# Two rows of attention factors: from TensorE transposes to small transfers through DRAM

## The chip, the cores and the metric

The kernel runs on one core of a Trainium2 chip. The metric is the device time of one execution in microseconds (us); less is better. Before the change it is 2583.25 us, the median of 3 runs from 2581.5 to 2585.15. The profiled execution has a span of 2584.1 us.

A core has five engines with a queue each: TensorE (PE: matmuls and transposes, into PSUM), VectorE (DVE), ScalarE (ACT), GpSimd (POOL) and SyncE (SP, which here only issues transfers). An engine runs its queue in order, and an instruction at its head that waits for a semaphore holds up all behind it. Transfers run on 16 DMA engines.

## What is computed

The input x is 32 graphs of 512 nodes with 256 features, in fp32, with one adjacency matrix for all. Per graph two layers follow each other, both added to x:

```
# layer 1, on layernorm(x):
out = relu(x @ mlp1_w + mlp1_b);  residual = out
out = elu(gat(relu(out), None, W_fc, a_fc)) + residual
out = relu(out @ mlp2_w + mlp2_b);  residual = out
out = relu(elu(gat(relu(out), adj, W_hand, a_hand)) + residual)
# where
def gat(inp, adj, W, a):
    h = inp @ W
    f1 = h @ a[:F, 0];  f2 = h @ a[F:, 0]
    e = leaky_relu(f1[:, :, None] + f2[:, None, :], 0.2)
    if adj is not None: e = where(adj > 0, e, -9e15)
    return elu(einsum('bij,bjf->bif', softmax(e, axis=2), h))
# layer 2, on layernorm(x): per head, softmax weights of 64 slices, sums of the
# nodes by them, attention among the 64 slice tokens, and back to the nodes
```

What matters here are f1 and f2, one number for each node. Matmuls leave them as a column: node on the partition, four tiles of 128 nodes. The matrix e needs one of the two as a column, and the other as a row of 512 that is the same on all 128 partitions. Getting from the column to that row is what the change is about.

## The kernel before, in words

The kernel handles the 32 graphs one after the other. A graph b passes through `front` (line 650), `middle` (757) and `back` (850), whose parts have names: load, norm1, mlp1, h, factors, p, pv, o1 (front); mlp2, h2, e, p2, pv2 (middle); norm2, w, sums, s1T, tokens, att, vo, gg, out (back). Parts of up to four graphs run at the same time, each in another stage.

The order of the queues is not the order of the program text. A `Recorder` takes every instruction down with a cost, and `order` plans them: each part has a due time in `TURNS`, and the instruction that can start and is due first goes next. `HEAD` and `TAIL` shift the due times of the first and last three graphs. `ISSUE`, `BEGIN`, `LAND`, `BEHIND` and `SWITCH` are what the plan takes for transfers and for changes of the matmul's shape. The resulting order is fixed; `emit` (line 281) issues it, so the profile gives line 283 for all, and one has to go by the tiles' names.

For graphs other than the first and last (`EDGES`), most transposes of big tiles don't go through TensorE. `flip` has VectorE transpose blocks of 32 × 32 into a stage, and `gather` (line 392) writes the stage to DRAM in four transfers and reads it back in one, all from SyncE's queue. In the first and last graph TensorE transposes them.

**factors** (line 682) and **p**: h comes with the columns f1 and f2. VectorE takes the maximum of f2 per partition (fm), TensorE transposes it, VectorE takes the maximum of that, f2m, over all nodes. Then sc = f1 + f2m (a column of 4 tiles), and TensorE spreads it: each of the four columns, repeated 128 times along the free axis, is transposed with the identity, which gives a row of 128 that is the same on all partitions. The row, in PSUM, is clamped twice, by VectorE and by ScalarE, into acb [128, 2, 512], and one exponential is taken of both halves. The column f1 in h is then overwritten by ones, so that the product pv gives the softmax's denominator as well. p builds pT, four tiles, with ScalarE multiplying and VectorE taking a maximum.

**pv**: TensorE multiplies pT with h. ELU follows, then `flip` and `gather` into o1T (o1), to which o0T is added, and mlp2 reads it.

**h2** (line 769): the second attention's h, with f1 and f2 in columns 256 and 257. TensorE spreads the four columns of f2 by transposes into PSUM as f2b. **e**: VectorE adds f2b, the column f1 and the mask, and goes on to leaky relu, the maximum and (ScalarE) the exponential; e is flipped and gathered into p2T (p2), and pv2 multiplies it with h2.

PSUM has five banks for matmuls (`mm`) and three for transposes (`tr`).

Of the kernel before, what the change touches and what calls it, by code (L numbers as in the profile page):

```python
# [7 lines left out]
F32 = mybir.dt.float32  # L8
I32 = mybir.dt.int32
AF = mybir.ActivationFunctionType  # L10
OP = mybir.AluOpType
# [2 lines left out]
ENGINES = ("tensor", "vector", "scalar", "gpsimd", "sync")  # L14

TURNS = {
    "load": -742.6, "norm1": -217.3, "mlp1": 743.3, "h": 847.3, "factors": 855.6, "p": 866.5,
    "pv": 872.7, "o1": 889.6, "mlp2": 900.8, "h2": 927.5, "e": 936.4, "p2": 556.1, "pv2": 977,
    "norm2": 1016, "w": 1035.7, "sums": 1041, "s1T": 1049, "tokens": 1120.9, "att": 78.2,
    "vo": 523.7, "gg": 243.7, "out": 1133,  # L20
}
PERIOD, SPARE = 91.72, 0.01

HEAD = (
    (243, -394, 14, 0, 2, 2, 38, -6, -57, -26, -306, -182, 126, -448, -107, 24, -145, -19, 984,
     -3, -394, 7),
    (-86, 191, -245, 43, 3, -49, 0, 187, -87, -24, 282, -45, 0, -140, -297, 924, -29, 7, 0, 21,
     -410, -757),
    (0, -12, 458, 33, 0, 23, -538, 0, -933, -32, 0, 724, -118, -26, -35, 487, -576, -1224, 125,
     0, -2, -1),  # L30
)
TAIL = (
    (9, -189, 0, 1, 0, 710, -45, -103, -26, -185, -41, 0, 510, -99, 6, 0, -90, 581, 0, 15, 209,
     0),
    (108, -81, 0, 1, -49, 31, -115, 202, -383, 0, 0, 6, 17, -64, 590, 1127, 26, -44, -68, 9,
     -11, 325),
    (207, 9, 610, 12, -3, 56, 140, -80, -21, 0, -139, -238, 66, 676, 2, -3, -3, 134, 14, 0, 68,
     -217),
)


# [4 lines left out]
P = 128  # L46
# [4 lines left out]
class Recorder:  # L51
# [2 lines left out]

    SIGNAL = 0.06
    DRAIN = 0.17
    ISSUE, BEGIN, LAND, BEHIND = 0.45, 1.2, 0.9, 2.7
    SWITCH = 0.14
    KEPT = 1
    AHEAD = 3  # L60

# [65 lines left out]
    def _cost(self, op, out, ins):  # L127


        def words(ap):  # L130
            return ap.size() // ap.ap[0][1]

        n = words(out)
        if op.method == "dma_start":
            side = next(ap for ap in (out, *ins) if ap.space != bass.MemoryType.DRAM)
            op.moving = out.size() * 4 / (215e3 if side.ap[0][1] <= P // 4 else 320e3)
            return self.ISSUE, 0.0
        if op.engine == "tensor":
            one = max(n / 1200 + 0.002, 0.109)
            if op.mode == (P, P // 2):  # L140
                one = max(n / 2400, 0.038)
            elif op.mode == (P // 2, P // 2):
                one = max(n / 4800, 0.022)
            return (one if op.method == "transpose" else 2 * one), self.DRAIN
        if op.engine == "scalar":
            pointers = sum(isinstance(op.kwargs.get(k), bass.AP) for k in ("bias", "scale"))
            return 0.06 + n / 1200 + 0.09 * pointers + 0.19 * ("accum_out" in op.kwargs), 0.12
        if op.engine == "vector":
            n = max([n] + [words(x) for x in ins])
            single = op.method in ("tensor_copy", "tensor_scalar")  # L150
            fast = single and all(x.space != bass.MemoryType.PSUM for x in ins)
            pointers = sum(words(x) == 1 for x in ins) if n > 1 else 0
            return 0.07 + n / (1920 if fast else 960) + 0.065 * pointers, 0.1
        if n < 16:
            return (0.1 if op.method == "memset" else 0.3 if op.method == "tensor_scalar" else 1.1), 0.1
        return 0.2 + n / (480 if op.method == "tensor_tensor" else 960), 0.1

    def _schedule(self, ops, key, spare):
# [35 lines left out]
        while len(done) < len(ops):  # L194
# [21 lines left out]
            if op.engine == "tensor" and op.mode != mode:  # L216
                t, mode = t + self.SWITCH, op.mode
            op.start, op.end = t, t + op.cost + op.lag
# [101 lines left out]
def adj_ffn_kernel(  # L320
# [26 lines left out]
    B, N, D = x.shape  # L347
    HID = mlp1_w.shape[1]
    HH = HID // 2
    NT = N // P  # L350
# [9 lines left out]
    nc = Recorder(tc.nc)  # L360
# [3 lines left out]
    dram = ctx.enter_context(tc.tile_pool(name="dram", bufs=1, space=bass.MemoryType.DRAM))  # L364

    def ts(i, n=P):
        return slice(i * n, (i + 1) * n)

    def new(name, shape, bufs=1, tag=None, dtype=F32):
        return sbuf.tile(list(shape), dtype, name=name, tag=tag or name, bufs=bufs)  # L370

    def mm_tile(shape):
        return psum.tile(shape, F32, tag="mm", name="mm", bufs=5)

    def tr_tile(shape):
        return psum.tile(shape, F32, tag="tr", name="tr", bufs=3)
# [4 lines left out]
    EDGES = (0, B - 1)  # L381
# [6 lines left out]
    def by_dma(what, b):  # L388

        return what in FLIPPED and b not in EDGES  # L390

    def gather(what, stage, dst):

        blocks, width = stage.shape[1:]
        scr = dram.tile([blocks, Q, P // Q, width], F32, name="scr", tag=f"scr_{what}", bufs=2)
        for a in range(P // Q):
            nc.sync.dma_start(
                scr[:, :, a, :].rearrange("c r j -> r c j"), stage[ts(a, Q), :, :]  # L400
            )
        nc.sync.dma_start(
            dst, scr.rearrange("(k c) r a j -> (c r) k (a j)", c=P // Q)
        )

    def swapped(cols):

        return cols.rearrange("p (t a i) -> p a t i", t=NT, i=Q)
# [7 lines left out]
    def small(name, shape):  # L416
        return new(name, shape, bufs=3)
# [8 lines left out]
    def load_x(b):  # L426
# [11 lines left out]
    ident = new("ident", [P, P])  # L438
    nc.gpsimd.memset(ident, 0.0)
    nc.gpsimd.affine_select(  # L440
        out=ident, in_=ident, compare_op=OP.not_equal, fill=1.0, base=0,
# [122 lines left out]
    for k in range(KD):  # L564
        pt = tr_tile([P, INNER])
# [33 lines left out]
    for p in range(NP):  # L599
        pv = mm_tile([P, D])  # L600
# [20 lines left out]
    def transpose_features(what, b, src, dst, swap):  # L621

        if by_dma(what, b):
            stage = new(what + "_stage", [P, D // Q, P], tag="stage4")
            for t in range(NT):
                flip(src[:, t, :D], stage[:, :, ts(t, Q)])
            gather(what, stage, dst)
            return
        for k in range(KD):
            pt = tr_tile([P, N])  # L630
            for t in range(NT):
                nc.tensor.transpose(pt[:, ts(t)], src[:, t, ts(k)], ident)
            if swap:
                nc.scalar.copy(dst[:, k, :].rearrange("p (a t i) -> p a t i", t=NT, i=Q), swapped(pt))
            else:
                nc.scalar.copy(dst[:, k, :], pt)
# [13 lines left out]
    def front(b):  # L650
# [21 lines left out]
        h = new("h", [P, NT, 2, HH + 1])  # L672
        for t in range(NT):
            for s in range(2):
# [4 lines left out]
                    )  # L679
                nc.scalar.copy(h[:, t, s, :], pm)  # L680
        f1, f2 = h[:, :, 0, HH], h[:, :, 1, HH]
        nc.step = "factors"

        fm = small("fm", [P, 1])
# [3 lines left out]
        f2m = small("f2m", [P, 1])  # L688
# [2 lines left out]


        beta = 1.0 - ALPHA
        sc = small("sc", [P, NT])
        nc.vector.tensor_scalar(sc, f1, f2m, None, op0=OP.add)
        ex = small("ex", [P, 2, NT])
        nc.vector.tensor_scalar(ex[:, 0], f2, f2m, None, op0=OP.subtract)
        nc.vector.tensor_scalar(ex[:, 1], f2, f2m, ALPHA, op0=OP.subtract, op1=OP.mult)
        nc.scalar.activation(ex, ex, AF.Exp)

        nc.vector.memset(f1, 1.0)

        pt = tr_tile([P, N])
        for i in range(NT):
            nc.tensor.transpose(pt[:, ts(i)], sc[:, i : i + 1].to_broadcast([P, P]), ident)
        acb = new("acb", [P, 2, N])
        nc.vector.tensor_scalar(acb[:, 0, :], pt, -beta, 0.0, op0=OP.mult, op1=OP.max)
        nc.scalar.activation(acb[:, 1, :], pt, AF.Relu, scale=beta)
        nc.scalar.activation(acb, acb, AF.Exp, scale=-1.0)

        nc.step = "p"
# [1 line left out]
        for j in range(NT):  # L713
# [5 lines left out]
                op0=OP.mult, op1=OP.max,  # L719
# [6 lines left out]
        for i in range(NT):  # L726
# [14 lines left out]
            pt = tr_tile([P, KH, P])  # L741
# [8 lines left out]
        if by_dma("u", b):  # L750
            gather("u", stage, o1T)
            for m in range(KH):
                o1 = o1T[:, m, :].rearrange("p (t a i) -> p t a i", t=NT, i=Q)
                nc.vector.tensor_tensor(o1, o1, swapped(o0T[:, m, :]), op=OP.add)
        return o1T

    def middle(b, o1T):
# [12 lines left out]
        h = new("h2", [P, NT, D + 2], tag="h" if b == B - 1 else None)  # L770
        for t in range(NT):
# [3 lines left out]
                    pm, o2T[:, k, ts(t)], wh[:, k, :], start=(k == 0), stop=(k == KD - 1)  # L775
                )
            nc.scalar.copy(h[:, t, :], pm)
        f2b = tr_tile([P, N])
        for j in range(NT):
            nc.tensor.transpose(f2b[:, ts(j)], h[:, j, D + 1 : D + 2].to_broadcast([P, P]), ident)  # L780
        if not by_dma("e", b):
            pt, f2b = f2b, new("f2b", [P, N], tag="acb")
            nc.scalar.copy(f2b, pt)
        nc.step = "e"
        pT = new("p2T", [P, NT, N], tag="pT" if b == B - 1 else None)
# [3 lines left out]
        for i in range(NT):  # L789
            e = new("e", [P, N], bufs=2)  # L790
# [11 lines left out]
            pt = tr_tile([P, NT, P])  # L802
# [7 lines left out]
        if by_dma("e", b):  # L810
            gather("e", stage, pT)
# [15 lines left out]
        for i2 in range(NT // 2):  # L827
            parts = []
            for s in range(2):
                i = 2 * i2 + s  # L830
# [218 lines left out]
    for b in range(B):  # L1049
        nc.age = b  # L1050
        back(b, middle(b, front(b)))
# [57 lines left out]
```

## Time and profile before

| | before |
|---|---|
| time, median of 3 | 2583.25 us |
| span of the profiled execution | 2584.1 us |
| TensorE busy | 2543.5 us (98%) |
| VectorE busy | 1992.3 us (77%) |
| ScalarE busy | 1075.3 us (42%) |
| GpSimd busy | 90.5 us (4%) |
| DMA moved | 375.9 MB, 145 GB/s on the mean |
| transposes of sc (f1; two more a graph by this name are the attention's) | 192 records, 43.9 us |
| transposes of h (f2) | 128 records, 24.2 us |
| clamp of acb by VectorE, from PSUM | 32 records, 692 ns each |
| clamp of acb by ScalarE, from PSUM | 32 records, 598 ns each |

How to read it: a matmul in fp32 shows as two records on TensorE, a transpose as one. Matmuls are pipelined, so the records overlap, and the busy time is the time in which one at least is in flight; what one costs the queue is the distance from its start to the next start. In the lists of groups and timelines, `out<-in` are the tiles' names without numbers: `tr<-ident,sc` is the transpose of sc by the identity. Waits are given as who waited, for whom, us in total, times, and the longest. In the list of transfers stand the issuing queue, how many, the size of one and the median us from the issue's start to the landing.

### The profile page before, as it was taken

The page shows a single profiled execution, that of the slowest core. Times are in us where ns is not written, and L with a number is a line of the kernel's source. Part 1 is how long each engine was busy: PE and PEld are TensorE (multiplying, and loading weights), DVE is VectorE, ACT ScalarE, POOL GpSimd, SP SyncE. Part 2 cuts the span into 40 slices and gives each one's busy share as a digit, 9 for nine tenths or more (in the row PEclk, how much of TensorE's full clock was granted, in tenths as well). Part 3 has the DMA queues.
Part 4 walks back from the last instruction along what each step waited for, and adds up shares of the span by engine and source line. Part 5 has one row for each costly group of instructions (what it writes and reads, how often), then busy time and mean ns, then how long its engine had stood idle before and what let it go on. Part 6 is the DMA issues. An engine that isn't in the chain of part 4 may idle for free.

```text
span 2584.1 us, 35267 instructions
## 1 busy us (share of the span) xinstructions
PE 2543.5 (98%) x12437; PEld 1863.3 (72%) x12437; DVE 1992.3 (77%) x4968; ACT 1075.3 (42%) x2009; POOL 90.5 (4%) x167
## 2 busy tenths in 40 slices
PE   7999999999999999999999999999999999999998
PEld 5777767776677777777776777767777677777776
DVE  6577777877778777788777788777887778877786
ACT  3443444433444334444334443344443344433442
POOL 0000000000000000000000000000000000000000
PEclk9999999999999999999999999999999999999999
DMA  5135455554455554555544555545545455554342
GB/s 177 53 87 153 114 156 171 155 163 128 136 176 162 157 149 124 168 172 150 162 133 138 175 161 158 147 122 171 164 148 160 124 155 171 155 165 137 114 123 82
DMA packets 465318, 375.90 MB, mean 145 GB/s; under 512 B 86004, under 2 KB 382068, under 8 KB 465142
## 3 DMA queue, kind: packets, MB, share of 16 engines
q1 hardware_dynamic: 463558, 372.59, 48.6%
q8 instruction: 99, 1.62, 0.3%
q10 hardware_dynamic: 1584, 1.05, 0.1%
q14 instruction: 77, 0.63, 0.1%
HBM read 198.45 MB, written 175.11 MB: 145 GB/s over the span
## 4 chain that ended last, share of the span: by engine, by line
PE 84%; DVE 7%; DMA 6%; ACT 1%; SPq 1%; issue 1%; POOL 0%; DVEq 0%; ACTq 0%
PE mm L283 81%; PE tr L283 3%; DMA o1T<-scr 2%; DMA scr<-u_stage 2%; SPq L283 1%; DVE s L283 1%; DVE s_stage L283 1%; DVE acb L283 1%; ACT acb L283 1%; DVE pT L283 1%; DVE u L283 1%; DMA w_raw<-scr 1%; DVE w L283 0%; DVE u_stage L283 0%; DMA p2T<-scr 0%
## 5 line engine op out<-in xcount | busy, mean ns | idle before, releaser
L283 PE MATMUL mm<-wfc,o0T 128*128 128x257 f32 x2048 | 509.8, 382 | 0.0
L283 PEld LDWEIGHTS mm<-wfc,o0T 128*128 128x128 f32 x2048 | 375.5, 189 | 141.7 <-issue 102.3
L283 PE MATMUL mm<-h,pT 128*128 128x257 f32 (+1 forms) x2048 | 462.1, 382 | 8.2 <-DVE pT L283 4.7
L283 PEld LDWEIGHTS mm<-h,pT 128*128 128x128 f32 x2048 | 383.2, 189 | 80.8 <-DVE pT L283 24.3
L283 ACT COPY h<-mm 128x257 f32<-128x257 f32 (+1 forms) x384 | 143.6, 374 | 375.9 <-PE mm L283 373.7
L283 PE MATMUL mm<-weff,xn2T 128*128 128x512 f32 x512 | 248.7, 592 | 0.6 <-ACT xn2T L283 0.6
L283 PE MATMUL mm<-xn,w 128*128 128x256 f32 x1024 | 247.5, 380 | 0.9 <-DVE ln_mv L283 0.8
L283 PE MATMUL mm<-xnT,w 128*128 128x512 f32 x512 | 239.1, 600 | 1.0 <-ACT m L283 0.6
L283 PE MATMUL mm<-o1T,w 128*128 128x512 f32 x512 | 227.6, 596 | 12.0 <-DVE o1T L283 10.5
L283 PE MATMUL mm<-h,p2T 128*128 128x257 f32 x1024 | 236.7, 380 | 1.1 <-DMA p2T<-scr 1.1
L283 PE MATMUL mm<-gg,wT 128*128 128x256 f32 x1024 | 237.5, 380 | 0.1
L283 PEld LDWEIGHTS mm<-gg,wT 128*128 128x128 f32 x1024 | 191.3, 190 | 40.3 <-issue 14.3
L283 PEld LDWEIGHTS mm<-h,p2T 128*128 128x128 f32 x1024 | 193.8, 190 | 30.8 <-DVE ln_mv L283 1.0
L283 PEld LDWEIGHTS mm<-xn,w 128*128 128x128 f32 x1024 | 185.1, 190 | 33.0 <-issue 3.9
L283 PEld LDWEIGHTS mm<-o1T,w 128*128 128x128 f32 x512 | 94.8, 190 | 128.2 <-issue 101.0
L283 ACT ACTIVATE u<-mm,rd 128x256 f32<-128x256 f32 x192 | 90.2, 470 | 217.9 <-DVE u_stage L283 85.9
L283 DVE STREAM_TRANSPOSE o_stage<-o2T 128x512 f32<-128x512 f32 x64 | 45.1, 708 | 160.3 <-ACT o2T L283 160.3
L283 DVE SCALAR_TENSOR_TENSOR e<-tr,h,mbias 128x512 f32<-128x512 f32 x120 | 86.6, 742 | 106.4 <-PE tr L283 106.3
L283 ACT ACTIVATE w<-w 128x512 f32<-128x512 f32 x128 | 80.7, 630 | 199.2 <-DVE w L283 199.2
L283 PEld LDWEIGHTS mm<-xnT,w 128*128 128x128 f32 x512 | 93.2, 191 | 83.4 <-issue 77.0
L283 ACT ACTIVATE m<-m 128x512 f32<-128x512 f32 x192 | 120.0, 625 | 66.9 <-DVE m L283 66.7
L283 DVE SCALAR_TENSOR_TENSOR u<-m,u 128x512 f32<-128x512 f32 x192 | 130.9, 682 | 18.8 <-ACT m L283 15.9
(140 smaller groups left out, 3466.0 us busy)
## 6 DMA issues: line engine op xcount, KB each, us to landing
scr<-xn_stage SPq DMA_DIRECT2D x240, 128.0 KB, 2.4
scr<-u_stage SPq DMA_DIRECT2D x120, 256.0 KB, 4.8
o1T<-scr SPq DMA_DIRECT2D x30, 1024.0 KB, 5.9
scr<-e_stage SPq DMA_DIRECT2D x120, 256.0 KB, 4.5
p2T<-scr SPq DMA_DIRECT2D x30, 1024.0 KB, 5.7
scr<-w_stage SPq DMA_DIRECT2D x120, 256.0 KB, 5.6
w_raw<-scr SPq DMA_DIRECT2D x30, 1024.0 KB, 5.6
x<-in_x_dram SPq DMA_DIRECT2D x32, 512.0 KB, 6.1
```

Of the source, the lines that this page charges most:

```text
L283: getattr(getattr(self.nc, op.engine), op.method)(*op.args, **op.kwargs)
```

## The change

The row f1b is no longer made by TensorE from sc, and f2b no longer by TensorE from h2, in the 30 graphs that are not first or last. A new helper, `spread`, issues two transfers from ScalarE's queue: the column of 512 words goes to a line in DRAM, and the line is read back by all 128 partitions at once. The second waits for the first to land. f1b is spread as soon as h is there, without f2m. f2m is added when VectorE clamps: one op on f1b makes −0.8 (f1 + f2m), and two relus on ScalarE make the two halves of acb from it. The overwriting of f1 by ones moves behind, since the transfer has to have read it. f2b lies in SBUF, in a buffer of its own.

The plan's constants are changed as well: a transfer from ScalarE's queue is taken to land 2.4 us after its issue (`ASIDE`), the other transfers' and small matmuls' costs are set anew, and `TURNS`, `HEAD` and `TAIL` are new. So the order of all parts is new too.

It is meant to take eight transposes a graph from TensorE, and their PSUM banks, and to leave the spreading to engines that have time.

```diff
 TURNS = {
-    "load": -742.6, "norm1": -217.3, "mlp1": 743.3, "h": 847.3, "factors": 855.6, "p": 866.5,
-    "pv": 872.7, "o1": 889.6, "mlp2": 900.8, "h2": 927.5, "e": 936.4, "p2": 556.1, "pv2": 977,
+    "load": 555.3, "norm1": 231.9, "mlp1": 708.7, "h": 730.5, "factors": 749.4, "p": 686.4,
+    "pv": 773.5, "o1": 784.2, "mlp2": 795.1, "h2": 803.4, "e": 808.3, "p2": 339, "pv2": 892.1,
...
-    ISSUE, BEGIN, LAND, BEHIND = 0.45, 1.2, 0.9, 2.7
-    SWITCH = 0.14
+    ISSUE, BEGIN, LAND, BEHIND = 0.45, 2.2, 0.0, 3.6
+    ASIDE = 2.4
+    SWITCH = 0.1
...
+    def spread(what, column, dst):
+
+        line = dram.tile([NT, P], F32, name="line", tag=f"line_{what}", bufs=2)
+        nc.scalar.dma_start(line.rearrange("t p -> p t"), column)
+        nc.scalar.dma_start(dst, bass.AP(tensor=line.tensor, offset=line.offset, ap=[[0, P], [1, N]]))
...
         f1, f2 = h[:, :, 0, HH], h[:, :, 1, HH]
+        if b not in EDGES:
+            f1b = new("f1b", [P, N])
+            spread("f1", f1, f1b)
...
-        sc = small("sc", [P, NT])
-        nc.vector.tensor_scalar(sc, f1, f2m, None, op0=OP.add)
         ex = small("ex", [P, 2, NT])
...
+        acb = new("acb", [P, 2, N])
+        if b in EDGES:
+            sc = small("sc", [P, NT])
+            nc.vector.tensor_scalar(sc, f1, f2m, None, op0=OP.add)
+            pt = tr_tile([P, N])
+            for i in range(NT):
+                nc.tensor.transpose(pt[:, ts(i)], sc[:, i : i + 1].to_broadcast([P, P]), ident)
+            nc.vector.tensor_scalar(acb[:, 0, :], pt, -beta, 0.0, op0=OP.mult, op1=OP.max)
+            nc.scalar.activation(acb[:, 1, :], pt, AF.Relu, scale=beta)
+        else:
+            nc.vector.tensor_scalar(acb[:, 0, :], f1b, f2m, -beta, op0=OP.add, op1=OP.mult)
+            nc.scalar.activation(acb[:, 1, :], acb[:, 0, :], AF.Relu, scale=-1.0)
+            nc.scalar.activation(acb[:, 0, :], acb[:, 0, :], AF.Relu)
         nc.vector.memset(f1, 1.0)
-
-        pt = tr_tile([P, N])
-        for i in range(NT):
-            nc.tensor.transpose(pt[:, ts(i)], sc[:, i : i + 1].to_broadcast([P, P]), ident)
-        acb = new("acb", [P, 2, N])
-        nc.vector.tensor_scalar(acb[:, 0, :], pt, -beta, 0.0, op0=OP.mult, op1=OP.max)
-        nc.scalar.activation(acb[:, 1, :], pt, AF.Relu, scale=beta)
         nc.scalar.activation(acb, acb, AF.Exp, scale=-1.0)
...
-        f2b = tr_tile([P, N])
-        for j in range(NT):
-            nc.tensor.transpose(f2b[:, ts(j)], h[:, j, D + 1 : D + 2].to_broadcast([P, P]), ident)
-        if not by_dma("e", b):
-            pt, f2b = f2b, new("f2b", [P, N], tag="acb")
+        if by_dma("e", b):
+            f2b = new("f2b", [P, N])
+            spread("f2", h[:, :, D + 1], f2b)
+        else:
+            pt, f2b = tr_tile([P, N]), new("f2b", [P, N])
+            for j in range(NT):
+                nc.tensor.transpose(pt[:, ts(j)], h[:, j, D + 1 : D + 2].to_broadcast([P, P]), ident)
             nc.scalar.copy(f2b, pt)
```

## The prediction

> **What bounds the kernel now.** I read the busy table first, then the chain that ended last, then the list of what TensorE waited for, then TensorE's timeline around the work that is changed.
>
> The busy table and the chain of the page:
>
> ```profile
> PE 2543.5 (98%) x12437; PEld 1863.3 (72%) x12437; DVE 1992.3 (77%) x4968; ACT 1075.3 (42%) x2009; POOL 90.5 (4%) x167
> ...
> PE 84%; DVE 7%; DMA 6%; ACT 1%; SPq 1%; issue 1%; POOL 0%; DVEq 0%; ACTq 0%
> ```
>
> TensorE is busy for 98% and carries 84% of the chain; VectorE has a fifth of its time free, ScalarE more than half. TensorE's clock is granted in full. So time saved on TensorE counts in full, unless it turns into a wait. TensorE's waits, in us in total, times, longest:
>
> ```profile
> PE mm L283 <- DVE o1T L283: 10.5, 10, 1.9
> PE tr L283 <- DVE xn L283: 9.8, 2, 8.3
> PE mm L283 <- DVE pT L283: 4.7, 4, 4.0
> ```
>
> They are few. But a busy TensorE is matmuls in flight, each reported some 170 ns longer than its share, so I also compared starts. The timeline of TensorE in one steady graph (start, us, then the work):
>
> ```profile
> 1264.80 0.27 PE L283 MATMUL tr<-ident,fm 128*128 128x128 f32 x1
> 1264.91 5.34 PE L283 MATMUL mm<-gg,wT 128*128 128x256 f32 x24
> 1270.09 1.89 PE L283 MATMUL mm<-xn,w 128*128 128x256 f32 x8
> 1271.82 0.27 PE L283 MATMUL tr<-ident,sc 128*128 128x128 f32 x1
> 1271.93 0.60 PE L283 MATMUL mm<-xn,w 128*128 128x256 f32 x2
> ...
> 1277.01 3.20 PE L283 MATMUL mm<-h,p2T 128*128 128x257 f32 x14
> 1280.35 2.12 PE L283 MATMUL mm<-h,pT 128*128 128x257 f32 x8
> ```
>
> A transpose is reported as 0.27 us but holds the next start back by 0.11 (1271.82 to 1271.93). Two records make a matmul: 5.18/12 = 0.432 us with 256 columns. The next max-transpose starts at 1343.45, so this graph took 78.65; over the steady graphs the median is 79.06. The same order laid out by starts without waits is 77.23. The missing 1.83 us a graph are, from starts later than their kind's median: 0.52 before the second MLP (it waits for o1T), 0.26 where pv first reads pT (here the next starts 3.34 us on, against 14 × 0.216 = 3.02), and about 1.05 of small steps at weight and array changes that will stay.
>
> **What the Trainium skill says.** "TensorE: Matmul & The Clock Gate", Part 4, puts a transpose at some 275 ns in a kernel; the trace has 272 as the record's length, but 110 as what the queue loses, and I price with 110. "VectorE: DVE Perf Modes", Why PSUM operands drop a tier, has one-input work on fp32 twice as fast from SBUF; the trace agrees: the clamp from PSUM takes 692 ns, a one-input op of the same 512 columns from SBUF 416. "DMA: Bandwidth & Descriptors", Issuing engines are not separate DMA queues: a transfer from ScalarE shares the same engines, only the issue is apart. Its Bandwidth section calls transfers under 64 KB bound by descriptors rather than bytes (its table is of another issuing path); this trace has a 2 KB load in words of 4 bytes that took longer than 16 KB in rows:
>
> ```profile
> xt<-in_x_dram SPq DMA_DIRECT2D x2, 256.0 KB, 2.9
> m<-in_L_ffn_W_x_dram SPq DMA_DIRECT2D x1, 256.0 KB, 4.0
> setup<-in_L_ffn_W_k_dram SPq DMA_DIRECT2D x2, 16.0 KB, 1.9
> b<-in_L_gnn_mlp_b_dram ACTq DMA_DIRECT2D x1, 2.0 KB, 3.9
> ```
>
> **The change part by part**, for the 30 graphs that are not the first or last.
>
> TensorE: 4 transposes of f1 and 4 of f2 go, 8 × 0.109 = 0.87 us a graph, 26.2 us in all. All of it is on the path.
>
> VectorE: the sum sc (0.22) goes, the clamp from PSUM (0.69) becomes a one-input op from SBUF (0.42): 0.5 us less of 62.3. e reads f2b from SBUF instead of PSUM: 746 against 742 ns, nothing. ScalarE: one more relu of 512 columns (0.60) and four issues. An issue from its queue in the first microseconds took 0.46 to 0.53, so 1.9; together 2.5 us onto 33.1 of 79. Nothing there is near full, so no cost by load, only by waiting.
>
> The transfers: two pairs a graph, a column of 512 words of 4 bytes to DRAM, then that line read to 128 partitions (256 KB). The trace has neither in the steady state. First half: between 1.9 (16 KB) and 3.9 (the 2 KB in words, beside the first loads); I take 3.3, nearer the upper since the words are the same. Second half: between 2.9 (256 KB beside few others) and 4.3 (the 256 KB row spread at the start, with others before it); I take 3.2. With 0.1 for the hand-over, a pair is 4.9, 6.6 or 8.3. Traffic: 60 × 0.25 MB = 15 MB on 376, 4%.
>
> What covers them. I laid TensorE's new order of one graph out with the measured distances between starts (0.432 us for 256 columns, 0.858 for 512), from the transpose of the maximum fm on; it is 76.36 long without waits:
>
> ```
>  0.00 tr fm, then 7 output products (gg,wT)   44.88 8 of the second MLP (o1T)
>  3.13 16 sums (xn,w)                          51.74 1 of w (weff,xn2T)
> 10.04 32 pv (h,pT)                            52.60 8 of h2 (wh,o2T)
> 23.87 16 pv2 (h,p2T)                          56.07 7 of w, 24 of h (wfc,o0T) mixed
> 30.78 tokens, first MLP, attention, 8 of h    72.47 9 output products, 76.36 the next tr fm
> ```
>
> f1: the last h matmul ends 13.9 us before pv (9 + 7 products of the output at 0.432, the transpose of the maximum, 16 sums). The chain is copy and drain 0.57, pair, clamp 0.42, two relus 1.2, the exponential of w 0.63 which stands between, exp 1.06, first pT 0.71 + 0.74: with the hand-overs 5.6 + pair = 10.5, 12.2, 13.9. It just fits. But the clamp heads VectorE's queue: behind it stand the add into the output, then the subtraction, sum and division of the last tile of w, 3.6 us until the sums can use it, and their 11th matmul, the first to read it, comes 11.35 us after h. Chain 0.57 + pair + 0.42 + 3.6 = 9.5, 11.2, 12.9: room of 1.9, 0.2 or minus 1.5. The fourth pT stands behind the s1 work, some 12.1 us after the clamp, and pv reads it at 19.1: 0.57 + pair + 0.42 + 12.1 = 18.0, 19.7, 21.4, so up to 2.3 short, 0.6 in the middle.
>
> f2: h2 ends at 56.1 of the layout; f2b is there 0.57 + pair later, 61.6, 63.3 or 65.0. VectorE has other work until 62.4. From its first e to the maximum of f2 of the following graph it has 13.2 us of work (four e at 0.66 + 0.60 + 0.60 + 0.63, and w between), and TensorE's transpose of that maximum stands at 76.36: VectorE is there at 75.6, 76.5, 78.2, so 0, 0.2 or 1.9 late. The reading of p2T has moved whole behind pv, so e's gather has room. The two shortfalls overlap, since a late maximum also delays the sums: 0, 0.6 or 2.3 together.
>
> ScalarE: the second transfer of a pair waits at the head of its queue for the first to land. For f2, behind it is one copy of h that is not due until TensorE is done with it; for f1 two exponentials stand between, which VectorE releases about when the line lands. I cost it at nothing: five PSUM banks hold TensorE up.
>
> The new turns: pv's end to the second MLP is 21.0 us in the new layout and was 19.7, so most of the 0.52 goes; the 0.26 before pv is replaced by the shortfall above. The rest of pv2's way to w is now 21.0 us instead of 30 (layout), and took 22.0 to the copied xn2T; there VectorE put tok and the attention between and the o1T gather held its 128 KB writes at 4.7 us, so it can stand or cost up to 1. I take 0.3.
>
> Sum per graph: 0.87 + 0.52 + 0.26 gone, 0.6 + 0.3 come: 0.75 less, × 30 = 22 us. 2583 − 22 = 2561. Start and end (TensorE idle 13 us in the first 80 and 9 in the last 124) have new turns too; I can't sign that, ±6.
>
> **Rivals.** *All is hidden*: pairs at 5 us. Then 1.65 − 0.1 = 1.55 a graph, 46 us: 2537. For it: 1.9 us for 16 KB; against: the words of 4 bytes. *The waits eat the gain*: pairs of some 7.3 us cost 1.3, and xn2T 0.4: 2583. *A transfer takes TensorE's place as the bound, slower*: pairs at 8.3 cost 2.3 a graph at pT and the maximum; 2.3 − 1.65 = +0.65, × 30 = +20: 2603. For it: 3.9 and 4.3 are measured, and e's writes and the 1 MB of p2T run at the moment of f1's pair; against: those figures come from the crowded first 12 us.
>
> **How the numbers follow.** Forecast 0.50, hidden 0.20, eaten 0.10, slower 0.20. Range: 2537 to 2598, from the hidden case to most of the slow one. Faster 0.71 (the forecast, the hidden one, a little of the eaten), same 0.08, slower 0.21.
>
> **What would show it.** 120 transposes fewer on each of sc and h (all but the first and last graph's); TensorE's period near 78.3; landing of the word column near 3.3 and of the spread row near 3.2; VectorE waiting for f2b and f1b by under 1 us each; TensorE waiting for pT or w by well under 1 us a graph. Pairs over 7.5 us, or xn2T turning up in TensorE's waits, make the prediction wrong on the slow side; f1b found landed when VectorE comes to it, on the fast side.

## The result, and the profile after

The changed kernel takes 3038.73 us, the median of 4 runs (3032.37 to 3042.29), against 2583.72 (4 runs as well) for the kernel before: a ratio of 1.1759, 95% interval 1.1738 to 1.1781. That is 455 us slower. The forecast was 2561, and even its slowest case was 2603.

The busy table and the chain of the page, after:

```profile
PE 2649.4 (87%) x12197; PEld 1916.4 (63%) x12197; DVE 1989.1 (66%) x4938; ACT 1079.9 (36%) x2039; POOL 86.1 (3%) x167
...
PE 52%; DMA 30%; DVE 11%; ACT 4%; issue 2%; SPq 0%; POOL 0%; DVEq 0%; ACTq 0%
PE mm L289 51%; DMA line<-h 19%; DMA f2b<-line 4%; DVE e L289 4%; DMA f1b<-line 4%; ACT acb L289 2%; PE tr L289 1%; DVE nmax L289 1%; DVE e_stage L289 1%; DVE w L289 1%; DMA scr<-xn_stage 1%; DVE w_stage L289 1%; ACT pT L289 1%; DVE mx L289 1%; DVE acb L289 0%
```

The 240 transposes are gone (12437 to 12197), and the chain, 84% TensorE before, is now 52% TensorE and 30% transfers. One of them, the column of words `line<-h`, is 19% of the span. The 446 us between the two spans (3030.5 and 2584.1) split in two: TensorE stands idle for 381.1 us (3030.5 − 2649.4) instead of 40.6, and is busy 105.9 us longer although it has less to do. The second part goes with the granted clock, 0.953 instead of 0.999: output products (gg,wT), 380 ns before, have a mean of 441.

The transfers of the changed kernel (out<-in, queue, number, KB each, median us from issue to landing):

```profile
scr<-e_stage SPq DMA_DIRECT2D x120, 256.0 KB, 8.3
r<-scr SPq DMA_DIRECT2D x32, 512.0 KB, 12.7
f1b<-line ACTq DMA_DIRECT2D x30, 256.0 KB, 4.5
f2b<-line ACTq DMA_DIRECT2D x30, 256.0 KB, 4.1
line<-h ACTq DMA_DIRECT2D x60, 2.0 KB, 10.5
```

The smallest transfer of the steady state, 2 KB, takes 10.5 us; the spread row of 256 KB takes 4.1 to 4.5. A pair is 14.6 to 15 us where 6.6 was forecast and 8.3 was the upper end. Two transfers that the change doesn't touch are late as well, r and the writes of e. Their lines before:

```profile
scr<-e_stage SPq DMA_DIRECT2D x120, 256.0 KB, 4.5
...
r<-scr SPq DMA_DIRECT2D x32, 512.0 KB, 3.7
```

What waited, over the whole kernel (engine, tile, what it waited for: us in total, times, longest):

```profile
ACT h L289 <- DMA line<-h: 220.8, 28, 9.6
...
DVE rs L289 <- issue: 163.6, 24, 7.1
...
PE tr L289 <- DVE fm L289: 121.8, 28, 7.6
...
DVE e L289 <- DMA f2b<-line: 88.9, 30, 8.9
PE mm L289 <- DVE ex L289: 86.1, 24, 5.8
...
PE mm L289 <- ACT h L289: 78.2, 48, 6.2
```

TensorE's own two largest waits are the transpose of the maximum fm and the sums (its matmul `mm<-xn,w`, put down to ex); the third is for copies of h on ScalarE. One steady graph tells how they come about. ScalarE's timeline (start, length, work, in brackets the idle time before and what ended it):

```profile
1457.24 0.38 ACTq L289 DMA_DIRECT2D line<-h  x1
...
1467.07 0.33 ACTq L289 DMA_DIRECT2D f2b<-line  x1
1467.43 0.37 ACT L289 COPY h<-mm 128x257 f32<-128x257 f32 x1 [7.66 <-DMA line<-h]
...
1481.35 0.38 ACTq L289 DMA_DIRECT2D line<-h  x1
...
1492.36 0.33 ACTq L289 DMA_DIRECT2D f1b<-line  x1
```

The second transfer can be issued only when the first has landed: 9.8 us for f2, 11.0 for f1. VectorE in the same stretch:

```profile
1471.83 1.42 DVE L289 SCALAR_TENSOR_TENSOR e<-f2b,h,mbias 128x512 f32<-128x512 f32 x2 [2.78 <-DMA f2b<-line]
...
1492.33 0.68 DVE L289 TENSOR_REDUCE rs<-w 128x8 f32<-128x512 f32 x1 [6.88 <-issue]
1492.36 0.06 DVE L289 MEMSET h<- 128x4 f32 x1
...
1496.51 0.49 DVE L289 TENSOR_SCALAR acb<-f1b,f2m 128x512 f32<-128x512 f32 x1 [1.15 <-DMA f1b<-line]
```

The 6.88 us put down to "issue" end at the moment when f1's column has landed. The write of ones over f1 (the MEMSET of h) is then the next in VectorE's queue, and it may not start before the transfer has read f1; the queue stands until the transfer is reported complete. And TensorE:

```profile
1467.86 2.00 PE L289 MATMUL mm<-wfc,o0T 128*128 128x257 f32 x8 [1.57 <-ACT h L289]
...
1476.12 4.15 PE L289 MATMUL mm<-gg,wT 128*128 128x256 f32 x18 [1.07 <-ACT h L289]
1484.91 0.48 PE L289 MATMUL tr<-ident,fm 128*128 128x128 f32 x1 [4.64 <-DVE fm L289]
1485.18 4.76 PE L289 MATMUL mm<-gg,wT 128*128 128x256 f32 x14
...
1494.75 5.38 PE L289 MATMUL mm<-xn,w 128*128 128x256 f32 x16 [3.95 <-DVE ex L289]
```

In this graph f2's pair costs 1.57 + 1.07 + 4.64 us, and f1's 3.95 and 0.56 more where the sums go on: 11.8. Over the steady graphs TensorE stands for 12.0 us a graph, against 0.7 before. The steady period grew by 15, from 79.1 to 94.0, and 30 times 15 is 450. The rest of the 15 comes with the clock: right behind the wait of 4.64 the trace has it at half of full speed for 3.4 us, and the 7 products from 1485.18 on (two records each, the next start at 1489.77) are 0.66 us apart instead of 0.43.

### The profile page after: what moved, and what is told of

It is laid out like the page before. It is cut to its first block, busy times and chain, and to the rows that moved or that the text cites. A ratio compares the mean times of both kernels' runs of the same rounds, so it can differ in the third digit from the quotient of the medians.

```text
span 3030.5 us, 34891 instructions
## 1 busy us (share of the span) xinstructions
PE 2649.4 (87%) x12197; PEld 1916.4 (63%) x12197; DVE 1989.1 (66%) x4938; ACT 1079.9 (36%) x2039; POOL 86.1 (3%) x167
## 4 chain that ended last, share of the span: by engine, by line
PE 52%; DMA 30%; DVE 11%; ACT 4%; issue 2%; SPq 0%; POOL 0%; DVEq 0%; ACTq 0%
PE mm L289 51%; DMA line<-h 19%; DMA f2b<-line 4%; DVE e L289 4%; DMA f1b<-line 4%; ACT acb L289 2%; PE tr L289 1%; DVE nmax L289 1%; DVE e_stage L289 1%; DVE w L289 1%; DMA scr<-xn_stage 1%; DVE w_stage L289 1%; ACT pT L289 1%; DVE mx L289 1%; DVE acb L289 0%
## 5 line engine op out<-in xcount | busy, mean ns | idle before, releaser
L289 PEld LDWEIGHTS mm<-wfc,o0T 128*128 128x128 f32 x2048 | 384.2, 192 | 196.9 <-issue 91.0
L289 PE MATMUL mm<-h,pT 128*128 128x256 f32 (+1 forms) x2048 | 454.8, 381 | 11.3 <-DVE pT L289 11.2
L289 PE MATMUL mm<-xn,w 128*128 128x256 f32 x1024 | 282.1, 431 | 124.5 <-DVE ex L289 86.1
L289 PEld LDWEIGHTS mm<-xn,w 128*128 128x128 f32 x1024 | 218.4, 219 | 181.0 <-issue 95.1
L289 PE MATMUL mm<-gg,wT 128*128 128x256 f32 x1024 | 287.3, 441 | 27.7 <-ACT h L289 26.9
L289 DVE TENSOR_REDUCE rs<-w 128x8 f32<-128x512 f32 x128 | 86.9, 679 | 338.2 <-ACT w L289 174.4
L289 PEld LDWEIGHTS mm<-gg,wT 128*128 128x128 f32 x1024 | 227.7, 228 | 75.1 <-ACT h L289 35.4
L289 ACT ACTIVATE e<-e,nmax 128x512 f32<-128x512 f32 x128 | 92.3, 721 | 332.1 <-DVE nmax L289 321.4
L289 DVE TENSOR_REDUCE mx<-mm 128x8 f32<-128x512 f32 x128 | 86.2, 674 | 129.5 <-PE mm L289 129.5
L289 DVE SCALAR_TENSOR_TENSOR e<-f2b,h,mbias 128x512 f32<-128x512 f32 x128 | 92.8, 745 | 90.6 <-DMA f2b<-line 88.9
```

What stands on the lines that cost most here:

```text
L289: getattr(getattr(self.nc, op.engine), op.method)(*op.args, **op.kwargs)
```

## The experiments

The question was why 2 KB land in 10 us, and whether that is the whole loss.

**1. The transfers alone, by layout.** This kernel leaves the whole computation out and only writes and reads small lines; each read-back waits for its write to land.

```
A: line[t, p]      <- f1        (as in the change)      512 words, adjacent
B: line[0, p]      <- one tile of f1                    128 words, adjacent
C: line[t, p, 16]  <- f1, word 0 of each 16             512 words, 64 bytes apart
D: line[t, p, 128] <- f1, word 0 of each 128            512 words, 512 bytes apart
E: line[p, t]      <- compact column                    128 pieces of 16 bytes
F: line[p, t]      <- f1                                512 words, grouped by row
G: line[j, a, i]   <- a tile of 128x32                  128 rows of 128 bytes
H: one SBUF partition <- one tile of f1                 128 words
```

> This kernel leaves out the whole computation: it only sends one column of h to DRAM (or to one partition) in eight layouts, one transfer at a time, each read back before the next is issued. Theory W (the 512 words of 4 bytes land late because they go into few lines of DRAM, each line written by several DMA engines in small pieces): the layout of the change 9 to 10 us; 128 words in one row 3 to 5; the same 512 words 64 or 512 bytes apart under 4; 512 words[...] under 5; 128 pieces of 16 bytes 4 to 6; 128 rows of 128 bytes under 3. Rival C (every small write to DRAM costs the same, wherever it goes): 512 words 9 to 10 us in all four layouts, 128 pieces of any size about 4. Rival B (it is contention with SyncE's transfers): all under 4 here.

ScalarE's timeline of that kernel; the landing is the start of the read minus the start of the write (A 9.8, C 2.2, E 1.4, G 2.1 us):

```profile
1.96 0.40 ACTq L72 DMA_DIRECT2D lineA<-h  x1
11.79 0.33 ACTq L58 DMA_DIRECT2D backA<-lineA  x1
...
27.26 0.38 ACTq L80 DMA_DIRECT2D lineC<-h  x1
29.44 0.38 ACTq L64 DMA_DIRECT2D backC<-lineC  x1
...
36.17 0.34 ACTq L88 DMA_DIRECT2D lineE<-col  x1
37.60 0.34 ACTq L58 DMA_DIRECT2D backE<-lineE  x1
...
52.66 1.08 ACTq L96 DMA_DIRECT2D lineG<-wide  x1
54.72 0.33 ACTq L58 DMA_DIRECT2D backG<-lineG  x1
```

Medians: A 9.9, B 6.9, C 2.0, D 2.0, E 1.5, F 6.5, G 2.0, H 1.9. With nothing beside it the column takes as long as in the kernel, so it isn't contention. The same 512 words 64 bytes apart take 2.0, so it isn't the number of words, not their size by itself, and not ScalarE's queue. Nor is it closeness by itself: in E and G pieces from different partitions lie next to each other as well, but pieces of 16 and 128 bytes. And 128 words into SBUF (H) take 1.9, where 128 words into DRAM (B) take 6.9. So it is single words of 4 bytes that lie close together in DRAM. Theory W expected less of B (3 to 5) and F (under 5) and more of E (4 to 6), so its picture of what happens inside isn't confirmed; what the experiment shows is which layouts are slow.

**2. How close, and what else is held up.** Again only transfers: the column with words 4, 8, 16, 32 and 64 bytes apart, and a write of 128 KB by SyncE beside the column.

```
for gap in (1, 2, 4, 8, 16): line[t, p, gap][:, :, 0] <- f1
big <- block                      (SyncE, just after line <- f1)
```

> This kernel leaves out the whole computation: it sends the same column of 512 words to DRAM with the words 4, 8, 16, 32 and 64 bytes apart, one after the other; then a store of 128 KB from SyncE's queue alone, beside the column with words 4 bytes apart, and beside the column with words 64 bytes apart. Theory W with the cost going by the number of words in the same 64 bytes: 10, 5 to 6, 3 to 4, 2.5, 2 us. If any sharing is enough: 10 for all but the last. The store: 2.5 us alone and beside the spaced column; 8 to 10 beside the dense column if the slow words hold up what is behind them on the DMA engines, 2.5 if they don't.

Spacing and landing: 4 bytes 7.9 to 8.1 us with nothing beside and 10.0 to 10.6 with the big write beside, 8 bytes 2.9 to 4.2, 16 bytes 2.4 to 3.0, 32 bytes 1.8 to 2.0, 64 bytes 1.8 to 2.2. From 32 bytes on nothing more is gained, and 8 and 16 bytes are quicker than expected (5 to 6 and 3 to 4). Why the adjacent column took 9.2 to 10.6 with nothing beside it in experiment 1 and 7.9 to 8.1 here isn't known. The write of 128 KB beside the words, first adjacent, then spaced (`linebigbeside` lands where `bigbackbeside` starts):

```profile
34.12 0.37 ACTq L83 DMA_DIRECT2D linebeside<-h  x1
34.32 0.32 SPq L85 DMA_DIRECT2D linebigbeside<-block  x1
44.51 0.32 SPq L88 DMA_DIRECT2D bigbackbeside<-linebigbeside  x1
...
47.54 0.37 ACTq L83 DMA_DIRECT2D linebeside<-h  x1
47.74 0.32 SPq L85 DMA_DIRECT2D linebigbeside<-block  x1
...
49.89 0.32 SPq L88 DMA_DIRECT2D bigbackbeside<-linebigbeside  x1
```

Over the four rounds that is 9.7 to 10.2 us beside adjacent words and 2.0 to 2.3 beside spaced ones. The write that was meant to run alone did not: in the first round it started 0.3 us after adjacent words and landed in 10.7, in the others it ran beside spaced words and took 2.1 to 2.3. So a transfer of another queue that starts just after the adjacent words lands about when they do. That fits r (12.7) and the writes of e (8.3) in the changed kernel.

**3. The changed kernel with the words 64 bytes apart.** All queues are in the same order, instruction by instruction; only the line's layout differs, and four small writes of zeros at the start are added. It changes the values: the row is still read as 512 adjacent floats, so f1b and f2b hold mostly zeros.

```
-        line = dram.tile([NT, P], F32, ...)
-        nc.scalar.dma_start(line.rearrange("t p -> p t"), column)
+        line = lines[what, nc.age % 2]                 # [NT, P, 16], zeroed at the start
+        nc.scalar.dma_start(line[:, :, 0].rearrange("t p -> p t"), column)
```

> The changed kernel with every queue in the same order, instruction by instruction; only the place in DRAM of each of the 512 words differs: they lie 64 bytes apart, in a line filled with zeros at the start. The row is read from the first 2 KB of it, so it holds the wrong numbers: the work is the same, the values of f1b and f2b are not. Theory W (words that share 64 bytes of DRAM): the column lands in 2 to 3 us, e's and r2's transfers return to 4.5 and 3.7, and the time falls to what the prediction's sum gives for a pair of 6.5 us, 2545 to 2590. Rival T (the new turns are weak themselves, as the 2658 of them with TensorE's transposes suggest): 2640 or more even so. Rival S (waiting on ScalarE's queue): 2620 to 2900.

2565.7 us (2554.8 to 2571.1), ratio 0.992 [0.9892, 0.9948].

```profile
r<-scr SPq DMA_DIRECT2D x32, 512.0 KB, 4.0
f1b<-linef ACTq DMA_DIRECT2D x30, 256.0 KB, 3.3
f2b<-linef ACTq DMA_DIRECT2D x30, 256.0 KB, 3.7
linef<-h ACTq DMA_DIRECT2D x60, 2.0 KB, 2.1
```

The column lands in 2.1, the pair in 5.4 to 5.8, r is back to 4.0. Of TensorE's waits, fm is 1.5 us in the whole kernel instead of 121.8. The steady period is 78.1; the forecast said near 78.3. So the addresses of the words are the whole slowdown, 473 us between two kernels whose queues are the same. Experiment 4 repeats it with the right values.

**4. The same order, and the column written as rows.** VectorE transposes the column in blocks of 32 just before each transfer, and 128 rows of 128 bytes go to DRAM. The added transposes are put in when the order is already fixed, so the rest of it stays as in the change.

```
-        line = dram.tile([NT, P], F32, ...)
-        nc.scalar.dma_start(line.rearrange("t p -> p t"), column)
+        line = dram.tile([Q, P // Q, Q], F32, ...)
+        rows = small(what + "T", [P, Q])
+        (at emission) nc.vector.transpose(rows, column, each tile repeated Q // NT times)
+        nc.scalar.dma_start(line.rearrange("j a i -> a j i"), rows)
```

> The queues of all engines in the order of the changed kernel, and the full result: before each column goes to DRAM, VectorE transposes it in blocks of 32 (0.2 us, 60 of them, the only instructions added), so that it is written as 128 rows of 128 bytes instead of 512 words. Theory W (the words that share 64 bytes of DRAM are the whole loss): the column lands in about 2.0 us as with spaced words, the time is that of the spaced words (2566) plus at most 60 x 0.2 = 12 us, 2560 to 2585, period 78 to 78.5; the 2690 of the rows with the same turns planned anew is then the plan's, not the transfers'. Rival V (the transpose in VectorE's queue holds it up until the last copy of h, and the rows cost what they cost before): 2640 to 2700, with VectorE waiting for h before the transposes.

2571.7 us (2566.0 to 2577.7), ratio 0.9952 [0.9941, 0.9963]: 12 us faster than the kernel before. ScalarE's timeline of a steady graph:

```profile
1246.29 0.55 ACTq L291 DMA_DIRECT2D line<-f2T  x1
...
1248.35 0.32 ACTq L291 DMA_DIRECT2D f2b<-line  x1
```

2.06 us from the write to the read that waits for it (2.00 for f1), where the words took 9.8 and 11.0. TensorE's largest wait left is another gather, 25.3 us for xnT. Theory W gave 2560 to 2585; rival V falls.

**5. Words as they were, but from a copy.** Is it the write of ones, which makes VectorE stand 163.6 us? Here VectorE copies the column first, so the ones can be written at once. Order and DRAM layout are those of the change.

```
+        kept = small(what + "k", [P, NT])
+        (at emission) nc.vector.tensor_copy(kept, column)
-        nc.scalar.dma_start(line.rearrange("t p -> p t"), column)
+        nc.scalar.dma_start(line.rearrange("t p -> p t"), kept)
```

> The changed kernel, the same order in every queue, the words still adjacent in DRAM; but each column leaves from a small copy that VectorE makes, so that the write of ones over f1 needs no longer wait until the column has left. The trace of the changed kernel has VectorE standing 163.6 us before the work right behind that write, with the maximum f2m and the sums on TensorE behind it (86.1 and 3.95 us in the graph looked at). Theory W (the late landing is the cause, this wait is one of the places where it is paid): the row f1b comes 4 us behind that write and pv needs it, so most of what the sums gain is lost again before pv: 2950 to 3030, TensorE waiting for pT instead of ex, landings still near 10. Rival M (the write of ones is what makes the change slow): 2560 to 2700.

3090.8 us (3087.6 to 3096.0), ratio 1.1964 [1.1945, 1.1984]: 52 us slower than the change, not faster; both numbers missed.

```profile
DVE acb L291 <- DMA f1b<-line: 245.5, 28, 10.2
ACT ex L291 <- DMA line<-f1k: 213.0, 25, 11.2
...
PE mm L291 <- DVE x L291: 104.7, 24, 6.2
```

The wait has moved a few instructions down VectorE's queue, to acb, which waits for f1b itself; the add into the output (x) and the rest of w stand behind it, and TensorE's sums now wait there. The write of ones isn't the cause, it only was the first place to pay. Why the copy costs 52 us more wasn't separated. Against experiment 4, which has one VectorE instruction in the same place and also frees f1, the difference is 519 us, for the form of the write alone.

**6. Rows, planned anew.** As experiment 4, but the transposes are known to the planner, which then orders all queues afresh; with the new turns, and with those of the kernel before.

```
     def spread(what, column, dst):
+        nc.vector.transpose(rows, column, each tile repeated)      # recorded, planned
-        nc.scalar.dma_start(line.rearrange("t p -> p t"), column)
+        nc.scalar.dma_start(line.rearrange("j a i -> a j i"), rows)
```

> The changed kernel, but VectorE transposes the column first, so that the transfer to DRAM moves 128 rows of 128 bytes in place of 512 words of 4 bytes; result and order as in the changed kernel. Theory W: the first half lands in 2.5 us, the pair in 7, and the time is that of the prediction's forecast or a little over, 2555 to 2600. Rival T (the new turns and the plan's constants are at fault): stays over 2900. Rival S (what costs is that ScalarE stands waiting for a landing at all, whatever its length): 2700 to 2900.

> The factors by rows of 128 bytes through DRAM, with the turns and the plan's costs of the kernel before (only the two small transfers priced at 2.4 us). If the new turns are needed to give the pair its room: 2600 to 2750, with TensorE waiting for pT and for the transposes of the maximum. If the turns don't matter once the column is quick: 2555 to 2585, that is 26 us of TensorE's transposes gone, less a small wait.

New turns: 2690.5 us (2686.9 to 2700.0), ratio 1.043 [1.0405, 1.0454], in none of the three expected ranges. Old turns: 2936.4 (2931.0 to 2939.3), ratio 1.1368 [1.1352, 1.1385], far above both expected ranges. In the first, VectorE's queue has all the rest of w ahead of pT, and ScalarE's has f1's column after the last exponential of e instead of before it; TensorE's largest wait:

```profile
PE mm L289 <- DVE pT L289: 77.9, 30, 6.9
```

With the old turns VectorE stands before f2's transposes, and the sums wait for w:

```profile
DVE f2T L286 <- ACT h L286: 280.0, 28, 10.7
...
PE mm L286 <- DVE w L286: 119.2, 28, 4.8
```

With the same form of transfer the kernel thus takes 2572, 2690 or 2936 us by the order around it: a quick pair is needed, but by itself it is not enough.

**7. The new turns with TensorE's transposes.**

```
-        if b not in EDGES: spread("f1", f1, f1b)       and the branch that uses f1b
-        if by_dma("e", b): spread("f2", h[:, :, D + 1], f2b)
+        transposes on TensorE in every graph, as before
```

> The changed kernel with its new turns and constants, but TensorE spreads f1 and f2 in all graphs as before. Theory W: near the kernel before, 2570 to 2620. Rival T: over 2900. If it is faster than before, the turns alone are a gain.

2658.2 us (2656.8 to 2659.3), ratio 1.0293 [1.0277, 1.0308], period 81.7: above the 2570 to 2620 of theory W, far below rival T. TensorE waits 45.5 us for w. With TensorE's transposes the new turns and constants, planned afresh, thus cost 76 us and not 455.

**8. One factor by words, the other by TensorE.** f2 alone, and f1 alone, each by undoing the other half of the diff as in experiment 7, and planned afresh.

> The changed kernel, but f1 is spread by TensorE again; f2 keeps its transfers. Theory W, with 14.9 us for a pair against some 7 of room on each path: about half of the loss stays, 2780 to 2850. If only f1's pair hurts: near 2590. Rival T: over 2900.

> The changed kernel, but f2 is spread by TensorE again; f1 keeps its transfers (words). If the two pairs add up on 2658 (turns alone), with 291 for f2's, then f1's is 90 and this gives 2750. If each pair costs by itself what its 14 us exceed its cover by, 7 us a graph for f1 by the prediction's layout: 2860. Rival T: near 2660.

f2 alone 2948.8 us (2946.7 to 2952.2), ratio 1.1419 [1.1402, 1.1436]; f1 alone 2821.0 (2816.0 to 2824.3), ratio 1.0921 [1.0905, 1.0938]. Neither expectation was right: f2 alone is far over the 2780 to 2850 of theory W, and f1 alone lies between its two numbers, 2750 and 2860. (That f2 alone falls into rival T's range doesn't speak for T, which experiments 3 and 7 exclude.) Over experiment 7 that is 291 and 163, and both together 381 (3038.7 − 2658.2): each pair costs by itself, f2's more, and part of it overlaps. With f2 alone TensorE waits 118.5 us for fm, as in the change; with f1 alone the wait for fm is gone and the sums wait 117.3 for w.

**9. ScalarE set free.** The second transfer of each pair is issued by GpSimd, which has the time, so ScalarE never waits for a landing.

```
-        nc.scalar.dma_start(dst, bass.AP(tensor=line.tensor, ...))
+        nc.gpsimd.dma_start(dst, bass.AP(tensor=line.tensor, ...))
```

> The changed kernel, but the second transfer of each pair is issued by GpSimd, so that ScalarE never stands waiting for the column to land. Theory W (latency on the path to e and to pT): still over 2900. Rival S (the copies of h that stand behind the waiting issue on ScalarE, 221 us of waits in the trace): falls under 2850.

3012.7 us (3009.8 to 3015.6), ratio 1.1665 [1.1648, 1.1682]. ScalarE waits for no transfer of the pair any more, and VectorE waits 244.0 us for f2b instead of 88.9. TensorE still waits for copies of h, 130.6 us. So freeing ScalarE gains 26 us, with a plan that differs in other places too; the length of the pair stays, and with it most of the loss.

**10. The planner is told.** The planner took 2.4 us for each transfer; here 9.6 for the column and 3.9 for the row.

```
-    ASIDE = 2.4
+    ASIDE = 9.6, 3.9
-                return self.ISSUE, self.ASIDE
+                return self.ISSUE, self.ASIDE[out.space != bass.MemoryType.DRAM]
```

> The changed kernel with the words as they are, but the planner told what the transfers take: 9.6 us for the column, 3.9 for the row (it took 2.4 for each). It can put other work between, but the maximum of f2 and the output bound f1's pair at some 14 us against 14.6 to 15. If most of the loss is queues in an order made for a short pair: 2620 to 2750. If it is the length of the pairs and the slow landing of what goes beside them (e writes and r): 2850 to 3020. No case is under 2600.

2991.6 us (2977.8 to 2993.0), ratio 1.1566 [1.1547, 1.1586], within the range for the pair's length.

```profile
r<-scr SPq DMA_DIRECT2D x32, 512.0 KB, 3.8
...
line<-h ACTq DMA_DIRECT2D x60, 2.0 KB, 10.0
```

r and the writes of e (5.0) land in time again and ScalarE hardly waits (8.9 us for f2b), yet TensorE now waits 139.1 us before its matmuls on h and pT, and the period is 91.1. Telling the truth to this planner wins 47 us; with the turns left as they were most of the loss remains. Turns searched anew for such a pair weren't tried.

## Why the prediction was wrong

**The failed step is a term of the sum: "First half: between 1.9 (16 KB) and 3.9 (the 2 KB in words, beside the first loads); I take 3.3".** It measured 10.5. Both ends were the wrong row of the list. The 3.9 was a read of adjacent words, and experiment 2 agrees with it: its reads of adjacent words landed in 2.1 to 3.8 us. Written to DRAM, the same words took 9.9 in experiment 1. The page listed only transfers of the kernel before, and none of them wrote adjacent words to DRAM from different partitions. So the upper bound was not a bound, and the range had no case past a pair of 8.3.

The Trainium skill, "DMA: Bandwidth & Descriptors", Specifications, says that below 512 bytes a transfer is done by read-modify-write. The size of a piece alone doesn't give the time here: 4 bytes took 2.0 us 64 bytes apart and 9.9 adjacent, and pieces of 16 bytes took 1.5. The section "Anatomy of one DMA" of the same page, which describes transfers issued by GpSimd and not by ScalarE as here, puts most of a transfer's fixed time into the receipt of the last byte in memory. The trace of experiment 1 agrees on where the time lies: the packets of the adjacent words (A) and of the spaced ones (C) all started 0.9 to 1.3 us after the issue, and A landed at 9.2 to 10.6, C at about 2.

**The rest of the sum held in part, and its 2561 beside 2565.7 is luck.** Experiment 3 has pairs of 5.4 to 5.8, where the forecast took 6.6. By the prediction's own layout no shortfall is left for such a pair, and its terms give 1.35 to 1.55 us a graph, that is 2537 to 2543. Measured were 2565.7, and a period of 78.1 instead of 79.1. The gain on TensorE is there (busy for 2515.3 us instead of 2543.5), and so is the room for the pairs (TensorE's waits are 1.5 us for fm and 2.5 for pT in the whole kernel). But TensorE stands for 53.7 us instead of 40.6: 14.9 of it for xnT (25.3 in experiment 4), a gather that the prediction didn't name, where it gave 0.3 a graph to xn2T; and the stretch from the last transpose of fm to the end takes 130.5 us instead of 123.0.

**The second half** was taken as 3.2 and was 4.1 to 4.5 in the changed kernel, 3.3 and 3.7 in experiment 3. That is small beside the first half.

**The places were right; that they overlap was wrong.** The prediction had f2b at 56.7 plus a pair of the layout, VectorE free for it at 62.4, and 13.2 us of work to the maximum: with a pair of 14.6 that makes the maximum 8.1 us late, and 7.3 were measured (1.57 + 1.07 + 4.64). For f1 it named the clamp at the head of VectorE's queue and the last tile of w behind it; experiment 5 shows just that (245.5 us). But it let the two shortfalls overlap. In ScalarE's queue f1's column stands behind exponentials of e, which need f2b: f1's pair begins when f2's is over, and the two waits add. An estimate shows the size of it: with pairs of 14.6 and 15.0 in the prediction's own sum, its largest shortfall is 9.0 (the fourth pT), and 9.0 + 0.3 − 1.65 = 7.65 a graph is 230 us. What is missing to 455 is, as far as the trace shows, the waits that add and the slower clock, to which it gave nothing; the two weren't taken apart by a run.

**Three things it left out.** ScalarE's wait "at nothing": TensorE waits 78.2 us for the copies of h behind it, though experiment 9, which removes it in an order planned afresh, gains only 26 us. The write of ones over f1, which must wait for the column to leave, was not listed among the new waits: 163.6 us of VectorE's time, though experiment 5 shows that its removal alone gives nothing. And the effect of the words on other transfers (r 3.7 to 12.7) was not foreseen; by experiment 10 the loss remains nearly as large when those land in time.

**The rivals.** "A transfer takes TensorE's place as the bound" was the right mechanism, with 0.20, but sized at 2603: its pair of 8.3 was the same wrong bound. The sign that it named for this side, pairs over 7.5 us, is what came. "All is hidden" had the right condition but not the right number: with pairs of 5.4 to 5.8 nearly all waits are gone (experiment 3), and the time is 2565.7, not 2537.

## What to carry to other kernels

Before a column is sent to DRAM, look at where its words land: single words of 4 bytes that become neighbours cost 10 us here and delay other transfers, while the same data spaced by 32 bytes or more, or first turned into rows of 128 bytes on VectorE (0.2 us), cost 2. Then look at the order once more: the same quick pair gave 2572 us in one order and 2936 in another. A row of the profile bounds an unknown transfer only if direction, piece size and neighbourhood agree; where none agrees, measure the transfer alone first. And ask for each tile that a transfer reads which later write to it must wait: that write may stand at the head of a busy queue.

## What the runs showed of the hardware

- The landing of 512 words of 4 bytes in DRAM by their spacing: 4 bytes 7.9 to 10.6 us (experiments 1 and 2), 8 bytes 2.9 to 4.2, 16 bytes 2.4 to 3.0, 32 bytes 1.8 to 2.0. A quarter of the words, adjacent, took 6.9, so the time grows much less than their number; 128 adjacent pieces of 16 bytes took 1.5. What in the memory or on the way to it causes this stays open.
- A write of 128 KB from another queue, begun 0.2 us after adjacent words, landed in 9.7 to 10.2 us; after spaced words, in 2.0 to 2.3.
- The granted clock is lower where TensorE stands long, but not in step with the sum of its idle time: 0.999 with 40.6 us idle, 0.984 with 116.8 (experiment 6, new turns), 0.953 with 381.1, 0.933 with 413.6 (experiment 5), but 0.946 with 316.0 (experiment 10) and 0.941 with 333.9 (experiment 9). In the changed kernel's trace the clock is either full or half, and half in 59 stretches, most of them 3.4 or 6.8 us long, 288.1 us together. In the graph shown it is half from 1484.9 and from 1495.2 on, for 3.4 us each, right behind the waits of 4.64 and 3.95 us, and not behind those of 1.57 and 1.07. TensorE's busy time is 105.9 us longer there, nearly a quarter of the loss. What decides when a stretch begins and how long it lasts wasn't tested.
